# A GraphSAGE layer pair on one core: the first eight edge groups of layer 1 gathered from x, and other loop ends

## The chip, the core and the metric

The kernel runs on one core of a Trainium2 chip. Its time is that of the device, in microseconds (us), as the median of several runs. A core has five engines with a queue of instructions each: TensorE (PE, with its weight loads shown apart as PEld), VectorE (DVE), ScalarE (ACT), GpSimd (POOL) and SyncE (SP). SP and ACT also issue DMAs, and so does POOL: its indirect DMAs gather rows of a table in DRAM by a list of indices. One profiled execution stands beside the runs.

## The reference

Nodes have 128 features; N is 12500 nodes, E is 200000 edges, sorted by destination.

```python
h    = jnp.maximum(_layernorm(x), 0.0)
w    = edge_weight_raw / jnp.maximum(wsum, EPS)[dst]
feat = jax.nn.relu(node_features @ W_pool + b_pool)
msg  = feat[src] * w[:, None]
neigh = jax.ops.segment_max(msg, dst, num_segments=N)
rst  = node_features @ W1_self + neigh @ W1_neigh + b1
h    = jax.nn.relu(rst / jnp.maximum(norm(rst), EPS))
neigh2 = segment_sum(h[src] * w[:, None], dst) / jnp.maximum(deg, 1.0)[:, None]
out  = jax.nn.relu(h @ W2_self + neigh2 @ W2_neigh + b2)
return x + out
```

Here `node_features` is the first `h`. Layer 1 takes, for each node, the largest message of its edges; layer 2 takes their sum.

## The kernel before

The kernel has three parts, and each is an order of instructions written out by hand.

**Preparation** (L426 to L473). x is held in SBUF in 98 tiles of 128 nodes, and a step works on four of them. Four stages of different steps lie in one turn of the loop: statistics of the layer norm on DVE (L462, L463), then the normalised rows with relu on ACT and their transposes on PE (L451, L453), then hT (the node features with features on partitions) and the product with W_pool (L438, L441), and last the table `feat`: bias on DVE (L430), relu on POOL (L433), store to `feat_d` in DRAM by SP (L434). `fr` has three buffers, so a relu waits for the store of three steps before. The loads of x are in SP's queue ahead of those stores. POOL also clears the SBUF that x leaves (L454). `edges1` prepares the weights and segment limits of 65536 edges at a time, `sources` the indices `srcT` (L410 to L417).

**Layer 1** (L646 to L760). Edges go in 391 groups of 512, the last one of 320. `gather` (L561) issues four indirect DMAs for a group, of 128 rows each, from `feat_d` into one of eight `gt` buffers. Every twelfth group has its first 128 rows fetched row by row by SP and ACT instead (class `Rows`, L501), in the eleven steps ahead of it; its `takes` says which groups. Step i of the loop scales the rows of group i by edge weight on ACT (L696), and PE transposes them to the PSUM tile `pm` (L697). For group i-1 DVE runs a scan over the 512 edges (L703), which takes the running maximum within each destination; `kt`, a row of `keep_d` broadcast to 128 partitions, restarts it where the destination changes. Two edges are joined into one (L711, L712), transposed back (L740), copied (L727), and for group i-4 a product with a selection matrix (L752) puts the last edge of each destination into a window of 48 nodes, `pa`, which ACT copies into `agg` (L745). The PSUM tile `pa` has one buffer. `turns` says at which step a tile of 128 nodes is complete; `nodes1` (L597) then multiplies it by W1_self and W1_neigh, normalises it, and stores it to `h_d`. Background work of the edges fills the loop by `side_step`.

**Layer 2** (L763 to L807) gathers from `h_d` in the same groups; every eighth has rows by SP and ACT. PE multiplies the gathered rows by a matrix of weights (L801), DVE adds the window to `agg` (L806), and `nodes2` ends with bias, relu, the addition of x and the store.

A gather is only issued when its `gt` buffer has been read by the group eight before it. A gather from `feat_d` also waits for all stores of that table, and one from `h_d` for all of that one.

What decides which group is taken row by row, and where a gather stands in POOL's queue:

```python
def takes(self, g):
    return g % self.every == 0 and self.every <= g < NG - 4
...
for j, k in chunks:
    if j == 0 and byrow and byrow.takes(g):
        continue
    nc.gpsimd.indirect_dma_start(
        out=gt[:k, j, :], out_offset=None, in_=table_d[:, :],
        in_offset=bass.IndirectOffsetOnAxis(ap=srcT[:k, t, j, r:r + 1], axis=0))
```

Of the kernel before, what the change touches and what calls it, by code (L numbers as in the profile page):

```python
# [18 lines left out]
P = 128  # L19
D = 128  # L20
# [10 lines left out]
BL = 8  # L31
XC = 8


@with_exitstack
def gnn_kernel(ctx, tc, x, src, dst, ew, w_pool, b_pool, w1s, w1n, b1, w2s, w2n, b2, out):
# [22 lines left out]
    RHO = N * G / E  # L59
    assert TAIL > 0 and TAIL % Q == 0 and E % SLOW_B == 0 and D == x.shape[1]  # L60

# [24 lines left out]
    rp = both.enter_context(tc.tile_pool(name="rows", bufs=1))  # L86
    gp = both.enter_context(tc.tile_pool(name="eg", bufs=8))
    prep = ExitStack()
# [55 lines left out]
    for t0 in range(2 * Q, HI, XC):  # L144
        load_x(t0, XC)

    def load_rest():
# [262 lines left out]
    def sources():  # L410
        for t in range(NT):
# [5 lines left out]
            yield  # L417


    first_edges = edges1(pq, 0)  # L420
    source_steps = sources()
    rest = load_rest()
    groups = list(node_groups())
    offs, rstds, pts, pfs = ({} for _ in range(4))
    for i in range(len(groups) + 3):
        at = [groups[i - k] if 0 <= i - k < len(groups) else None for k in range(4)]  # L426
        if at[3]:
            t0, n = at[3]
            fb = wk.tile([P, Q, D], F32, name="fb")
            nc.vector.tensor_tensor(fb[:, :n, :], pfs.pop(i - 3)[:, :n, :],  # L430
                                    bp_all[:, None, :].to_broadcast([P, n, D]), OP.add)
            fr = wk.tile([P, Q, D], F32, name="fr", bufs=3)
            nc.gpsimd.tensor_scalar(fr[:, :n, :], fb[:, :n, :], 0.0, None, op0=OP.max)  # L433
            nc.sync.dma_start(feat_d[t0 * P:(t0 + n) * P, :].rearrange("(q p) d -> p q d", p=P),  # L434
                              fr[:, :n, :])
        if at[2]:
            t0, n = at[2]
            nc.scalar.activation(hT[:, t0:t0 + n, :], pts.pop(i - 2)[:, :n, :], AF.Copy)  # L438
            pf = pfs[i - 2] = ps.tile([P, Q, D], F32, name="pf")
            for q in range(n):  # L440
                nc.tensor.matmul(pf[:, q, :], hT[:, t0 + q, :], W["pool"], start=True, stop=True)  # L441
        if at[1]:
# [27 lines left out]
        if i >= 6:  # L470
            next(rest, None)
        if i >= len(groups) - 4:
            next(source_steps, None)  # L473
    for steps in (first_edges, rest, source_steps):
        for _ in steps:
            pass
# [13 lines left out]

    def edges_of(g):

        ne = G if g < GF else TAIL
        return *divmod(g, P), ne, [(j, min(P, ne - j * P)) for j in range(-(-ne // P))]

    def pairs_of(g):
# [4 lines left out]
    class Rows:  # L501
# [5 lines left out]

        def __init__(self, pool, table_d, every, share):
            self.pool, self.every, self.share = pool, every, share
            self.bytes = table_d[:, :].bitcast(U8).rearrange("n b -> (n b)")  # L510
            self.tiles, self.index, self.plan = {}, {}, {}
            self.ri = pool.tile([64, P], I32, name="ri", bufs=1)
            assert sum(n for _, n, _ in share) == P
            for g in range(every, NG - 4, every):
                first = g - every - 1
                at = 0
                for eng, n, rb in share:
                    for s in range(n // rb):
                        turn = max(first + s * every // (n // rb), 0)
                        self.plan.setdefault(turn, []).append((g, eng, at, rb))  # L520
                        at += rb
            self.turn(-2)
            self.turn(-1)

        def takes(self, g):
            return g % self.every == 0 and self.every <= g < NG - 4

        def turn(self, i):

            for g, lead, step in ((i + self.every + 2, -1, self.shift), (i + self.every + 3, -2, self.load)):  # L530
                if i == lead:
                    step(self.every)
                elif i >= 0 and g > self.every and self.takes(g):
                    step(g)
# [25 lines left out]

    def gather(pool, table_d, g, byrow=None):  # L561
        t, r, ne, chunks = edges_of(g)
        gt = pool.tile([P, Q, D], F32, name="gt")
        for j, k in chunks:
            if j == 0 and byrow and byrow.takes(g):
                continue
            nc.gpsimd.indirect_dma_start(  # L567
                out=gt[:k, j, :], out_offset=None, in_=table_d[:, :],
                in_offset=bass.IndirectOffsetOnAxis(ap=srcT[:k, t, j, r:r + 1], axis=0))
        return gt  # L570

    def turns(behind):
# [19 lines left out]

    def linear(po, t, nT, self_w, neigh_w):
        nc.tensor.matmul(po, hT[:, t, :], W[self_w], start=True, stop=False)
        return nc.tensor.matmul(po, nT, W[neigh_w], start=False, stop=True)  # L595

    def nodes1(wk, ps, t, nT, store=True):  # L597

        po = ps.tile([P, D], F32, name="pn")
        linear(po, t, nT, "1s", "1n")  # L600
        yield
# [28 lines left out]
    def nodes2(wk, ps, t, nT, xr):  # L630

        po = ps.tile([P, D], F32, name="pn")
        linear(po, t, nT, "2s", "2n")
        yield
# [11 lines left out]
    with tc.manual_schedule(), tc.tile_pool(name="ew", bufs=3) as wk, \  # L646
            tc.tile_pool(name="ep", bufs=2, space=PSUM) as ps:
        AHEAD = 4
        jobs = [(due, job(lambda: ps.tile([P, Q, P], F32, name="pq", bufs=1), t)) for due, job, t in background()]
# [9 lines left out]

        gts, kts, pms, scs, sels, prs, rws, pas = ({} for _ in range(8))  # L660
        turn = turns(6)
        busy = {}

        def keep_rows(g):
            ne = edges_of(g)[2]
            kts[g] = wk.tile([P, G], BF16, name="kt", bufs=AHEAD + 3)
            nc.sync.dma_start(kts[g][:, :ne], keep_d[g:g + 1, :ne].to_broadcast([P, ne]))  # L667

# [6 lines left out]

        for g in range(AHEAD):
            keep_rows(g)
        carry = NEG
        byrow = Rows(wk, feat_d, 12, [(nc.sync, 96, 8), (nc.scalar, 32, 4)])
        for i in range(max(turn) + 6):  # L680
            byrow.turn(i)
            byrow.rows(i, nc.sync)
            node_stage(5)
            if i + AHEAD < NG:
                keep_rows(i + AHEAD)
            if i < NG:
                gts[i] = gather(gp, feat_d, i, byrow)

            if i < NG:
                t, r, ne, chunks = edges_of(i)  # L690
                gs = wk.tile([P, Q, D], F32, name="gs", bufs=2)
                pms[i] = ps.tile([P, G], F32, name="pm")
                gt = gts.pop(i)
                for j, k in chunks:
                    rows_j = byrow.tile(i) if j == 0 and byrow.takes(i) else gt[:k, j, :]
                    nc.scalar.activation(gs[:k, j, :], rows_j, AF.Copy, scale=ewT[:k, t, j, r:r + 1])  # L696
                    nc.tensor.transpose(pms[i][:, j * P:j * P + k], gs[:k, j, :], ident[:k, :k])  # L697

            g = i - 1
# [29 lines left out]
            node_stage(4)  # L729
            if i in turn:  # L730
                n = turn[i]
                st = nodes1(wk, ps, n, agg[:, n * P:(n + 1) * P])
                next(st)
                busy[i + 1, 1] = st
            g = i - 2
            if 0 <= g < NG:
                prs[g] = ps.tile([P, Q // 2, D], F32, name="pr")
                sc = scs.pop(g)
                for j, k in pairs_of(g)[3]:
                    nc.tensor.transpose(prs[g][:k, j, :], sc[:, j * P:j * P + k], ident)  # L740

            g = i - 5
            if 0 <= g < NG:
                at = window_at(mybir.EngineType.Activation, g)
                nc.scalar.activation(agg[:, bass.ds(at, LW)], pas.pop(g), AF.Copy)  # L745
            g = i - 4
            if 0 <= g < NG:
                chunks = pairs_of(g)[3]
                pas[g] = ps.tile([P, LW], F32, name="pa", bufs=1)
                rows, sel = rws.pop(g), sels.pop(g)  # L750
                for j, k in chunks:
                    nc.tensor.matmul(pas[g], rows[:k, j, :], sel[:k, j, :], start=j == 0,  # L752
                                     stop=j == len(chunks) - 1)
            node_stage(2)
            byrow.rows(i, nc.scalar)
            if i % 3:
                side_step()
# [5 lines left out]
    with tc.manual_schedule(), tc.tile_pool(name="ew2", bufs=3) as wk, \  # L763
            tc.tile_pool(name="ep2", bufs=3, space=PSUM) as ps:
        iota = ps.tile([P, LW], F32, bufs=1)
        nc.vector.tensor_copy(iota, cols[:, 0, :])
        nc.vector.memset(agg, 0.0)
        gts, ss, pas, xrs = ({} for _ in range(4))
        turn = turns(3)
        late = None  # L770
        byrow = Rows(wk, h_d, 8, [(nc.sync, 64, 8), (nc.scalar, 64, 8)])
        for i in range(max(turn) + 2):
# [22 lines left out]
            if 0 <= g < NG:  # L795
# [3 lines left out]
                for j, k in chunks:  # L799
                    rows_j = byrow.tile(g) if j == 0 and byrow.takes(g) else gt[:k, j, :]  # L800
                    nc.tensor.matmul(pas[g], rows_j, s[:k, j, :], start=j == 0,  # L801
                                     stop=j == len(chunks) - 1)
            g = i - 2
            if 0 <= g < NG:
# [123 lines left out]
```

## Time and profile before

| | us |
|---|---|
| median of 3 runs | 3939.56 (3939.38 to 3942.92) |
| the profiled execution | 3936.91 |
| its span | 3935.1 |
| first gather from feat_d | 95.30 |
| last gather from feat_d | 2007.19 |
| first gather from h_d | 2033.27 |
| last gather from h_d | 3923.95 |

A line of the page's groups names the program line, the engine and operation, what is written and read, the shape and the number of instructions; behind the first bar come the busy time and the mean of one in ns, behind the second the idle time of the engine ahead of it and what ended it. In the timeline a line has its start, its duration, and in square brackets how long its engine was idle before and what ended that. "issue" is time in which an engine waited for nothing that the profile shows. A gather's time on POOL ends before its rows land: the last one of layer 2 starts on POOL at 3923.95, is over there at 3924.85, and PE reads its rows at 3926.31.

### The profile page before, as it was taken

How to read it: one execution, taken by the hardware profiler on the slowest of the kernel's cores; microseconds unless marked ns; L12 is line 12 of the kernel's file. 1: busy time of each engine (PE TensorE's matmuls, PEld its weight loads, DVE VectorE, ACT ScalarE, POOL GpSimd, SP SyncE). 2: the span in 40 equal slices, each digit the busy share in tenths (PEclk: the TensorE clock that was granted, in tenths of full speed). 3: DMA queues.
4: the chain of work that ended last, by engine and by line, in shares of the span. 5: the costliest groups of instructions: out<-in, count | busy, mean ns of one | idle time of the engine just before them, and what ended most of it. 6: DMA issues, size and time to landing. Idle time of an engine off the chain costs nothing.

```text
span 3935.1 us, 55137 instructions
## 1 busy us (share of the span) xinstructions
PE 2156.9 (55%) x8349; PEld 1760.9 (45%) x8349; DVE 1664.5 (42%) x4708; ACT 808.7 (21%) x2947; POOL 2925.7 (74%) x3105
## 2 busy tenths in 40 slices
PE   6446546555556545545545555555555555555555
PEld 4335435444445434444444444444444444444444
DVE  7556656666656656655652222122122222122221
ACT  6334334334334334334320000000000000000000
POOL 5777777777777777777757777777777777777776
PEclk8555565555555555555555555555555555555555
DMA  6233333333333333333322222222222222222222
GB/s 168 76 85 84 86 86 85 85 85 84 85 85 84 85 85 84 85 85 84 84 61 62 63 62 61 62 62 62 62 62 63 62 62 61 62 62 62 62 62 58
DMA packets 245792, 295.43 MB, mean 75 GB/s; under 512 B 71023, under 2 KB 195518, under 8 KB 245424
## 3 DMA queue, kind: packets, MB, share of 16 engines
q0 software_dynamic: 97472, 199.75, 18.7%
q1 hardware_dynamic: 139024, 89.04, 8.5%
q10 hardware_dynamic: 8928, 3.03, 0.3%
q14 instruction: 296, 2.42, 0.2%
q8 instruction: 72, 1.18, 0.1%
HBM read 271.77 MB, written 19.77 MB: 74 GB/s over the span
## 4 chain that ended last, share of the span: by engine, by line
DMA 23%; POOL 23%; issue 17%; SPq 9%; PE 9%; DVE 8%; ACT 5%; ACTq 5%; POOLq 0%; DVEq 0%
POOL gt L567 23%; DMA gt<-h_d,srcT 14%; SPq L556 6%; PE pm L697 4%; DVE pm L703 4%; ACTq L556 3%; DMA ga<-feat_d 3%; DMA kt<-keep_d 3%; ACT gs L696 3%; SPq L552 2%; DMA ri<-in_src 1%; ACTq L552 1%; PE pa L752 1%; DMA gt<-feat_d,srcT 1%; SPq L667 1%
## 5 line engine op out<-in xcount | busy, mean ns | idle before, releaser
L567 POOL DMA_INDIRECT gt<-feat_d,srcT x1531 | 1446.1, 945 | 469.5 <-issue 376.4
L567 POOL DMA_INDIRECT gt<-h_d,srcT x1515 | 1429.5, 944 | 487.3 <-issue 389.5
L801 PE MATMUL pa<-s,gt 128*128 128x48 f32 x3030 | 966.6, 423 | 827.6 <-DMA gt<-h_d,srcT 736.2
L801 PEld LDWEIGHTS pa<-s,gt 128*128 128x128 f32 x3030 | 757.0, 312 | 1038.5 <-DMA gt<-h_d,srcT 819.5
L697 PE MATMUL pm<-ident,gs 128*128 128x128 f32 x1563 | 481.2, 440 | 896.0 <-DVE sc L712 472.8
L697 PEld LDWEIGHTS pm<-ident,gs 128*128 128x128 f32 x1563 | 287.3, 197 | 1030.0 <-ACT gs L696 471.0
L806 DVE TENSOR_TENSOR agg<-pa,agg 128x48 f32 x391 | 81.2, 208 | 1438.8 <-PE pa L801 1025.2
L703 DVE TENSOR_TENSOR_SCAN pm<-kt,carry,pm 128x512 f32<-128x512 bf16 x390 | 498.6, 1279 | 231.3 <-PE pm L697 116.9
L696 ACT ACTIVATE gs<-gt,ewT 128x128 f32<-128x128 f32 x1531 | 495.6, 391 | 269.0 <-DMA ga<-feat_d 187.7
L752 PEld LDWEIGHTS pa<-sel,rows 128*128 128x128 f32 x1564 | 352.5, 311 | 35.9 <-ACT agg L745 34.4
L752 PE MATMUL pa<-sel,rows 128*128 128x48 f32 x1564 | 356.6, 374 | 3.5 <-ACT agg L745 1.2
L740 PE MATMUL pr<-ident,sc 128*128 128x128 f32 x782 | 236.2, 403 | 1.9 <-DVE sc L712 1.9
L542 DVE TENSOR_SCALAR ri<-ri 1x128 int32<-1x128 int32 x80 | 18.6, 233 | 512.3 <-DMA ri<-in_src 504.7
L720 DVE TENSOR_SCALAR sel<-cols,lastT,invT 128x48 f32<-128x48 f32 x782 | 211.4, 324 | 0.0
L712 DVE COPY_PREDICATED sc<-kt,pm 128x256 f32<-128x256 int16 x391 | 172.9, 442 | 13.3
L740 PEld LDWEIGHTS pr<-ident,sc 128*128 128x128 f32 x782 | 163.4, 218 | 2.2 <-issue 1.3
L711 DVE COPY sc<-pm 128x256 f32<-128x256 f32 x391 | 162.0, 414 | 0.0
L783 DVE TENSOR_TENSOR s<-hit,w2T 128x192 f32<-128x192 f32 x391 | 139.8, 357 | 13.5
L727 ACT ACTIVATE rows<-pr 128x256 f32<-128x256 f32 x392 | 142.3, 363 | 2.6 <-PE pr L740 2.4
L781 DVE TENSOR_TENSOR hit<-iota,locT 128x192 f32<-128x192 f32 x391 | 139.1, 356 | 0.8
L745 ACT ACTIVATE agg<-pa 128x48 f32 x391 | 78.6, 201 | 169.1 <-PE pn L595 164.8
L607 ACT ACTIVATE sq<-r 128x128 f32<-128x128 f32 x98 | 29.8, 304 | 401.9 <-DVE r L603 401.9
(149 smaller groups left out, 1395.7 us busy)
## 6 DMA issues: line engine op xcount, KB each, us to landing
kt<-keep_d SPq DMA_DIRECT2D x390, 128.0 KB
ga<-feat_d SPq DMA_DIRECT2D x3072, 0.5 KB
ga<-h_d SPq DMA_DIRECT2D x3072, 0.5 KB
ga<-h_d ACTq DMA_DIRECT2D x3072, 0.5 KB
gt<-feat_d,srcT POOLq DMA_INDIRECT x1531
gt<-h_d,srcT POOLq DMA_INDIRECT x1515
ga<-feat_d ACTq DMA_DIRECT2D x1024, 0.5 KB
h_d<-h SPq DMA_DIRECT2D x98, 64.0 KB
```

The costliest lines, as they stand in the source:

```text
L556: eng.dma_start(ga[r + k:r + k + 1, :], self.bytes[None, bass.ds(at[k], 4 * D)])
L567: nc.gpsimd.indirect_dma_start(out=gt[:k, j, :], out_offset=None, in_=table_d[:, :], in_offset=bass.IndirectOffsetOnAxis(ap=srcT[:k, t, j, ...
L696: nc.scalar.activation(gs[:k, j, :], rows_j, AF.Copy, scale=ewT[:k, t, j, r:r + 1])
L697: nc.tensor.transpose(pms[i][:, j * P:j * P + k], gs[:k, j, :], ident[:k, :k])
L703: nc.vector.tensor_tensor_scan(pm[:, :ne], kt[:, :ne], pm[:, :ne], carry, op0=OP.add, op1=OP.max)
L711: nc.vector.tensor_copy(sc[:, :ne // 2], two[:, :, 1])
L712: nc.vector.copy_predicated(sc[:, :ne // 2], new[:, :, 1], two[:, :, 0])
L720: nc.vector.tensor_scalar(sels[g][:k, j, :], cols[:k, 1, :], lastT[:k, t, j, r:r + 1], invT[:k, t, j, r:r + 1], op0=OP.is_equal, op1=OP.mult)
L727: nc.scalar.activation(rws[g][:k, j, :], pr[:k, j, :], AF.Copy)
L740: nc.tensor.transpose(prs[g][:k, j, :], sc[:, j * P:j * P + k], ident)
L752: nc.tensor.matmul(pas[g], rows[:k, j, :], sel[:k, j, :], start=j == 0, stop=j == len(chunks) - 1)
L801: nc.tensor.matmul(pas[g], rows_j, s[:k, j, :], start=j == 0, stop=j == len(chunks) - 1)
```

## The change

Groups 0 to 7 of layer 1 no longer use the table. During the preparation POOL gathers the rows of x themselves for their edges, two gathers in each step from step 2 on, into the eight `gt` buffers. These rows then go through layer norm, relu, transpose, the product with W_pool, bias and relu by themselves, as [feature x edge] tiles: group 0 at the end of the preparation, groups 1 to 7 in the first steps of layer 1. The edge weights come as rows broadcast to all partitions, and DVE multiplies by them. So gathers from `feat_d` begin with group 8. To have indices at that time, `sources` runs its first pass in steps 0 and 1.

```diff
+    bp_col = rp.tile([P, 1], F32)
+    nc.sync.dma_start(bp_col, b_pool[:, None])
...
+    def raw_stats(r):
+        mv = rp.tile([P, Q, 2], F32, name="raw_mv", bufs=2)
+        for q in range(Q):
+            st = rp.tile([P, 6], F32, name="raw_st", bufs=2)
+            nc.vector.bn_stats(st, gts[r][:, q, :])
+            nc.vector.bn_aggr(mv[:, q, :], st)
+        rstd = rp.tile([P, Q], F32, name="raw_rstd", bufs=2)
+        nc.scalar.activation(rstd, mv[:, :, 1], AF.Sqrt, bias=eps)
+        raws[r] = mv, rstd
+
+    def raw_rows(get, r):
+
+        mv, rstd = raws.pop(r)
+        nc.vector.reciprocal(rstd, rstd)
+        off = rp.tile([P, Q], F32, name="raw_off", bufs=2)
+        nc.vector.scalar_tensor_tensor(off, mv[:, :, 0], -1.0, rstd, op0=OP.mult, op1=OP.mult)
+        pt = raws[r] = get()
+        for q in range(Q):
+            nc.scalar.activation(gts[r][:, q, :], gts[r][:, q, :], AF.Relu, bias=off[:, q:q + 1],
+                                 scale=rstd[:, q:q + 1])
+            nc.tensor.transpose(pt[:, q, :], gts[r][:, q, :], ident)
+
+    def raw_product(get, r):
+
+        nc.scalar.activation(gts[r], raws.pop(r), AF.Copy)
+        pf = raws[r] = get()
+        nc.tensor.matmul(pf.rearrange("p q n -> p (q n)"), W["pool"],
+                         gts.pop(r).rearrange("p q n -> p (q n)"), start=True, stop=True)
...
-        if i >= len(groups) - 4:
+        if i == 1:
+            bias_rows = split_bias()
+        if i < 2 or i >= len(groups) - 4:
             next(source_steps, None)
+        if i >= 2:
+            n = 2 if i < len(groups) else len(raw_chunks)
+            for r, j in raw_chunks[:n]:
+                gts[r] = gather(gp, x, r, only=j, gt=gts.get(r))
+            raw_chunks = raw_chunks[n:]
+        k = i - len(groups)
+        if k == 1:
+            raw_rows(pq, 0)
+        if k == 2:
...
+        if k in (0, 1):
+            raw_stats(k)
```

The table's bias goes to PE: `split_bias` splits b_pool into three bf16 parts on DVE once (eight small operations), and one matmul of three rows adds them in PSUM ahead of the product. The relu leaves POOL: DVE does it, in every fourth step ACT, straight from PSUM to `fr`.

```diff
-            fb = wk.tile([P, Q, D], F32, name="fb")
-            nc.vector.tensor_tensor(fb[:, :n, :], pfs.pop(i - 3)[:, :n, :],
-                                    bp_all[:, None, :].to_broadcast([P, n, D]), OP.add)
+            pf = pfs.pop(i - 3)
             fr = wk.tile([P, Q, D], F32, name="fr", bufs=3)
-            nc.gpsimd.tensor_scalar(fr[:, :n, :], fb[:, :n, :], 0.0, None, op0=OP.max)
+            if i % 4 == 3:
+                nc.scalar.activation(fr[:, :n, :], pf[:, :n, :], AF.Relu)
+            else:
+                nc.vector.tensor_scalar(fr[:, :n, :], pf[:, :n, :], 0.0, None, op0=OP.max)
...
+            nc.tensor.matmul(pf[:, :n, :], ones_r[0:3, :P], bias_rows[0:3, :n, :], start=True, stop=False)
             for q in range(n):
-                nc.tensor.matmul(pf[:, q, :], hT[:, t0 + q, :], W["pool"], start=True, stop=True)
+                nc.tensor.matmul(pf[:, q, :], hT[:, t0 + q, :], W["pool"], start=False, stop=q == n - 1)
```

In layer 1 the first eight steps take the raw groups, with `pq` as the one PSUM tile for their transposes and products:

```diff
+        weight_rows(0)
+        keep_rows(0)
+        keep_rows(2)
         carry = NEG
-        byrow = Rows(wk, feat_d, 12, [(nc.sync, 96, 8), (nc.scalar, 32, 4)])
+        byrow = Rows(wk, feat_d, 12, [(nc.sync, 96, 8), (nc.scalar, 32, 4)], 24, NG - 16)
...
+            if i < FIRST:
+                pm = pms[i] = ps.tile([P, G], F32, name="pm")
+                w = ws.pop(i).rearrange("p q n -> p (q n)")
+                if i == 0:
+                    nc.vector.tensor_tensor(pm, gts.pop(0).rearrange("p q n -> p (q n)"), w, OP.mult)
+                else:
+                    nc.scalar.activation(pm, raws.pop(i).rearrange("p q n -> p (q n)"), AF.Relu, bias=bp_col)
+                    nc.vector.tensor_tensor(pm, pm, w, OP.mult)
+                if i + 1 < FIRST:
+                    weight_rows(i + 1)
+                    raw_rows(pq, i + 1)
...
+            if i + 1 < FIRST:
+                raw_product(pq, i + 1)
+            if i + 2 < FIRST:
+                raw_stats(i + 2)
```

Rows by SP and ACT are now for groups 24, 36 and so on up to 372. `keep_rows` loads two groups' rows with one DMA, every second step. At the end of layer 1 the window copies of the last steps move ahead of other work, a node tile is begun after the window's product rather than before, `pa` of every second of the last groups lies in the `pq` bank, and the W1_self halves of the last two node tiles run ahead of their turn into a bank of their own. In layer 2 the set-up of `Rows` moves ahead of the clearing of `agg`, and the W2_self halves of the last two tiles are computed at step NG - 1:

```diff
+                if g >= NG - 5 and g % 2 and not jobs:
+                    pas[g] = ps.tile([P, Q, P], F32, name="pq", bufs=1)[:, 0, :LW]
+                else:
+                    pas[g] = ps.tile([P, LW], F32, name="pa", bufs=1)
...
+            if i >= NG - 2:
+                begin_node()
+            n = HI - 2 + i - NG
+            if n in (HI - 2, HI - 1) and turn.get(i + 5) == n:
+                own[n] = ps.tile([P, G], F32, name="pm")[:, :D]
+                linear_own(own[n], n, "1s")
...
+            if i == NG - 1:
+                for n in (HI - 2, HI - 1):
+                    own[n] = ps.tile([P, D], F32, name="pn")
+                    linear_own(own[n], n, "2s")
```

## The prediction

> **What bounds the kernel now.** I read the page first, then POOL in order of time, then the stretches where POOL has no gather. The page's parts 1 and 5:
>
> ```profile
> span 3935.1 us, 55137 instructions
> PE 2156.9 (55%) x8349; PEld 1760.9 (45%) x8349; DVE 1664.5 (42%) x4708; ACT 808.7 (21%) x2947; POOL 2925.7 (74%) x3105
> ...
> L567 POOL DMA_INDIRECT gt<-feat_d,srcT x1531 | 1446.1, 945 | 469.5 <-issue 376.4
> L567 POOL DMA_INDIRECT gt<-h_d,srcT x1515 | 1429.5, 944 | 487.3 <-issue 389.5
> ```
>
> POOL is busiest, and almost all of it is gathers of 945 ns with about 0.30 us of "issue" before each. The timeline of POOL, with first and last gathers of layer 1 and the first of layer 2, shows whether anything interrupts them:
>
> ```profile
> 95.30 1.16 POOL L567 DMA_INDIRECT gt<-feat_d,srcT  x1 [2.75 <-DMA feat_d<-fr]
> 96.77 0.94 POOL L567 DMA_INDIRECT gt<-feat_d,srcT  x1 [0.30 <-issue]
> ```
> ```profile
> 2007.19 0.91 POOL L567 DMA_INDIRECT gt<-feat_d,srcT  x1 [0.30 <-issue]
> 2033.27 0.95 POOL L567 DMA_INDIRECT gt<-h_d,srcT  x1 [25.17 <-DMA ri<-in_src]
> ```
>
> From 95.30 to 2007.19 there are 1530 steps: 1.2496 us each, which is duration plus issue and nothing else. Layer 2, 2033.27 to 3923.95, gives 1.2488 over 1514 steps. So the span is five terms: 95.3 of preparation, 1531 gathers, a hole of 25.17, 1515 gathers, 10.25 of tail. Only what changes one of these counts; work on DVE, ACT and PE inside a layer is covered as long as it frees the eight gt buffers (8 x 4 x 1.25 = 40 us ahead).
>
> **Gathers removed from layer 1.** Groups 0 to 7 leave the loop: 32 gathers. Rows by sync and scalar are now taken for groups 24 to 372 (30) instead of 12 to 384 (32), which gives 2 back. 1531 - 32 + 2 = 1501, so 30 x 1.2496 = **-37.5**. Layer 2 takes the same groups as before.
>
> **The 32 gathers in the preparation.** From step 2 on, two per step: 2.5 us beside a 0.52 us memset is 3.0 of a step of about 3.3 (reciprocals of rstd at 17.68, 20.94, 24.27), and the relu of 1.49 us leaves POOL. They end at step 17 of 27, and only raw_stats at step 25 reads them, so they are hidden with seven steps to spare. Their traffic is not quite free: the DMA share is 0.95 to 1.09 until 30 us, while x is loaded at 301 GB/s, and some 8 gathers of 64 KB fall there: 0.5 MB, 1.7 us later for the loads and all that SP has queued behind them.
>
> Here the Trainium skill speaks against the change. Its page "SBUF — State Buffer", section "A bandwidth-pool intuition that's wrong (but worth ruling out)", says that descriptors of a DMA from GpSimd wait while a VectorE operation in a two-port mode holds the shared port: 3100 ns for one that takes 620 alone. Gathers now go beside the DVE-heavy preparation. By that figure a step would hold 2 x 3.4 + 0.5 = 7.3 us, 16 steps 117 us, and the first gather of the table would come near 130 instead of 103: the whole gain gone. The row says otherwise: layer 1 has 782 tensor_scalars SBUF to SBUF in f32 (sel, 324 ns), of the kind that the page names, beside 1531 gathers of median 944 and at most 1179 ns. I take the row.
>
> **Preparation, its end.** DVE, ACT and the waits of SP up to 95 us:
>
> ```profile
> L462 DVE BATCH_NORM_STATS2 st<-agg 128x6 f32<-128x128 f32 x98 | 26.1, 266 | 0.9 <-DMA agg<-in_x 0.9
> L463 DVE BATCH_NORM_AGGREGATE mv<-st 128x2 f32<-128x6 f32 x98 | 17.8, 182 | 3.4
> L430 DVE TENSOR_TENSOR fb<-pf,b 128x512 f32<-128x512 f32 x24 | 16.3, 681 | 6.2 <-PE pt L453 2.5 <-POOL fr L433 2.4 <-PE pf L441 1.3
> ```
> ```profile
> 30.18 1.48 POOL L433 TENSOR_SCALAR fr<-fb 128x512 f32<-128x512 f32 x1 [6.62 <-DMA feat_d<-fr]
> ```
>
> DVE sets the pace (17.98 us busy of 20 from 40 to 60). The reader sees at 30.18 that the fourth fr waited for the first feat_d store, which SP issues at 26.00, behind the x loads. POOL took this wait before, and DVE only 2.4 us of it. Now DVE writes fr itself and meets it at step 6. It gets there about 24.4 (23.67 before, + 1.4 for split_bias, which is 8 small operations, about 2.0 us less a 0.6 idle, - 0.65 for a relu on ACT). The store comes 1.7 + 0.4 (bp_col) later, lands near 32.2, and fr ends at 33.0. Step 8 before ended at 32.4; now 33.0 + 5.7 - 0.65 = 38.1: **+5.7**. From there every fourth relu goes to ACT, which has 5 us of 20 free: four times 0.65, of which I count 2.0: **-2.0**. The bias matmul goes to PE, which waits for ACT there: nothing (at most 25 x 0.3 if PE were late). At the end the relu on POOL (1.48) goes, but the sqrt of raw_stats(0) stands ahead of the last hT on ACT, and four raw relus (1.65) ahead of the last fr: the store is issued near 93.7 rather than 92.6: +1.1. The table is complete at 94.66 + 4.8 = 99.5.
>
> **A new wait at the start of layer 1.** The buffer of gather 8 is gts[0], read by DVE in group 0 together with weight_rows(0), whose place in SBUF is free only when the last feat_d store has landed. So: 99.5, + 2.7 for 256 KB (kt lands in 2.9 to 3.1 in the chain), + 0.67 multiply, + 0.2 = 103.1. First gather: **+7.8** in all. Behind it on POOL is every gather. Bounds: +3.5 (no DVE stall at step 6) and +13.
>
> **The raw groups as a pace.** Gather g for 9 to 15 waits until raw group g - 8 is through its matmul. One loop of it: four relus 1.65, transpose 0.45, copy 0.65, matmul of 512 columns in two passes (pf: 8 x 128 columns in 1.16 at full clock, 1.8 at the granted 0.53), relu 0.65, hops 0.3, multiply and scales 1.0: 6.5. By DVE: stats 4 x 0.40, scan with its copies 2.2, sel 0.5, multiply and scales 1.0, sqrt and relu on ACT between 1.0: 6.3. POOL needs 5.0. Gathers 10 to 15 wait 1.5 each: 6 x 1.5 = 9, with a little at the start **+9.5**. Bounds 0 (hops overlap) and 28 (a pace of 9). Afterwards the loop needs about 3.3 to 4.4 us a group and catches up.
>
> **The hole between the layers.** 25.17 before. In the timeline ACT waits for rows by sync of group 384 so long that six groups stand behind it when POOL ends at 2008.10:
>
> ```profile
> 2000.22 0.40 ACT L696 ACTIVATE gs<-ga,ewT 128x128 f32<-128x128 f32 x1 [15.11 <-DMA ga<-feat_d]
> ```
>
> The last gs begins at 2014.19; without a backlog it would at 2008.1 + 1.5, so 4.6 go. Then the order at the end: window copies ahead, pa in two banks, own products of the last two node tiles early. Counted down the dependences: gs, transpose, scan, copies 4.0 after POOL's end, pr, rows, pa, copy 6.7, two products, r, norm, h, store 12.8. Queues in between I put at 3: 16, **-9.2** (bounds 13 and 21). Pairs of keep rows halve their issues (0.36 each on SP), hidden. In layer 2 the set-up of the rows by sync moves ahead of the 10.55 us memset on DVE; DVE is the consumer there and POOL is 40 us ahead, so this is nothing; without that cover it would be a gain, since those rows could start 10 us earlier. The eight weight loads of 256 KB stand in SP's queue between keep rows; their price shows only in the first, above.
>
> **Tail.** PE runs 2s before 2n for two tiles after the last add; the first halves go ahead: **-0.65** of 10.25.
>
> **Sum.** +7.8 + 9.5 - 37.5 - 9.2 - 0.65 = -30.0; span 3905.1. The profiled execution took 3936.91 (span + 1.8), the median of the runs is 3939.56; I put the difference to the median: **3909.5**.
>
> **Rivals.** (a) The start hides better: first gather +4, raw groups +2, hole 16: -41, **3898**. For it: ACT and PE have slack; against: SP's queue and the single pq bank are serial. (b) Raw groups at 9 us, POOL held 28 instead of 9.5: **3928**. For it: eight hops between three engines in each, and two queues with work between; against: the rows sum to 6.5. (c) Slower: the same place, one mechanism. DVE and ACT wait for each other within a raw group (sqrt in ACT's queue ahead of the relu that DVE waits for), and the single pq makes transposes and product strictly serial; at 12 us a group POOL is held 49: **3949**. It decides from 5 + 39.5 / 7 = 10.6 us on; twice as many hops as I count would be needed. (d) The change does not do what it says: srcT of the first rows late, or gathers held by the port: the start moves to 130 and about 3 is gained, **3937**.
>
> **Chances.** Forecast (3898 to 3920) 0.58; (a) 0.12; (b) 0.17; (d) and the like 0.05; (c) 0.08. A change of 0.2% (8 us) is about what can be told from none. Faster 0.87, within 0.05, slower 0.08. Range 3893 to 3927.
>
> **What would show it.** 1501 gathers of feat_d at 1.25; first of them at 103; 32 gathers of x at 944 ns between 13 and 65; waits of POOL for PE before gathers 10 to 15 of 1.5 us; a hole of 16; 10.25 to 9.6 at the end. Wrong it is if POOL waits after group 16, or if the raw groups take 9 us and more.

## The result and the profile after

| | kernel before | changed kernel |
|---|---|---|
| median, us | 3942.49 (6 runs, 3939.38 to 3947.13) | 3922.11 (6 runs, 3919.01 to 3924.24) |
| ratio | | 0.9945, interval 0.9935 to 0.9955 |
| profiled execution, us | 3936.91 | 3919.01 |
| its span, us | 3935.1 | 3917.2 |

The changed kernel is 0.55% faster: 20.4 us between the medians, 18.0 us between the two spans (3935.14 and 3917.18). The forecast was 30.

The page of the changed kernel, parts 1 and 5. The columns are those of the page before.

```profile
span 3917.2 us, 54274 instructions
PE 2182.0 (56%) x8390; PEld 1775.6 (45%) x8390; DVE 1675.8 (43%) x4795; ACT 826.5 (21%) x2978; POOL 2898.7 (74%) x3082
...
L434 POOL DMA_INDIRECT gt<-h_d,srcT x1515 | 1433.2, 946 | 478.9 <-issue 402.0
L434 POOL DMA_INDIRECT gt<-feat_d,srcT x1501 | 1421.0, 947 | 478.9 <-issue 350.7
```

POOL is still the busiest engine, with the 1501 gathers of `feat_d` that were counted. Its timeline (start, duration, engine, line; in brackets the idle time before and what ended it) shows the five terms of the span again: preparation, gathers, hole, gathers, tail.

```profile
103.15 0.95 POOL L434 DMA_INDIRECT gt<-feat_d,srcT  x1 [9.98 <-DVE raw_off L458]
...
115.09 0.95 POOL L434 DMA_INDIRECT gt<-feat_d,srcT  x1 [1.99 <-PE pq L469]
...
149.22 0.95 POOL L434 DMA_INDIRECT gt<-feat_d,srcT  x1 [2.22 <-PE pq L469]
...
1992.09 0.91 POOL L434 DMA_INDIRECT gt<-feat_d,srcT  x1 [0.30 <-issue]
2009.62 0.96 POOL L434 DMA_INDIRECT gt<-h_d,srcT  x1 [16.62 <-issue]
```

The table of `feat` is gathered from 103.15 on. At seven places from gather group 9 to 15 POOL then stands for PE (`pq` L469, the product of a raw group). Normal idle before a gather is 0.30, so each bracket less 0.30 is lost: 0.25 at group 9, 1.69 three times, 1.92 three times, 11.1 us together. After 149.22 POOL waits for no other engine in layer 1. The hole is 16.62 in place of 25.17.

With both traces the difference of the spans can be written out, term by term:

| term | forecast, us | traces, us | how the trace gives it |
|---|---|---|---|
| start of the table's gathers | +7.8 | +7.85 | 103.15 - 95.30 |
| raw groups as a pace | +9.5 | +11.1 | the seven waits |
| 30 fewer gathers | -37.5 | -37.5 | 30 x 1.2496 |
| hole between the layers | -9.2 | -8.55 | 16.62 - 25.17 |
| tail | -0.65 | +1.8 | from the end of the last gather to the end of the span: 12.12 against 10.29 |
| step from gather to gather | 0 | +7.3 | layer 1 without its waits 1.2519 against 1.2496, layer 2 1.2513 against 1.2488, over 1500 and 1514 steps |
| sum | -30.0 | -18.0 | |

So the waits and counts that were named are there, most of them in their sizes. Most of the 12 us that are missing stand in two rows that the forecast held at nothing or had with the other sign: the step of the gathers and the tail.

**The gathers of x in the preparation.** POOL's timeline, the first and the last of the 32:

```profile
15.82 1.11 POOL L434 DMA_INDIRECT gt<-in_x,srcT  x1 [0.17 <-issue]
...
70.73 0.94 POOL L434 DMA_INDIRECT gt<-in_x,srcT  x1 [0.30 <-issue]
```

After the first one they take 0.94 to 0.95 us each, beside DVE's work of the preparation, and are over at 71.7. The first `raw_stats` reads such rows at 91.82.

**The start.** First SP's queue, then DVE's, from the timeline:

```profile
13.91 13.63 SPq L136 DMA_DIRECT2D agg<-in_x  x8
27.59 0.36 SPq L148 DMA_DIRECT2D bp_col<-in_L_gnn_b_pool  x1
28.05 0.39 SPq L505 DMA_DIRECT2D feat_d<-fr  x1
```
```profile
32.67 0.69 DVE L504 TENSOR_SCALAR fr<-pf 128x512 f32<-128x512 f32 x1 [7.49 <-DMA feat_d<-fr]
```

These rows show the queue in which the first store of the table waits: the last of the loads of x, then `bp_col`, then the store, at 28.05. The fourth `fr` has to wait for that store's buffer. It was POOL that stood there before; now it is DVE, idle for 7.49 us, with the statistics of all later tiles behind it. At the other end of the preparation DVE's multiplication for raw group 0 waits for the weight rows, whose load SP issues at 98.70. SP's queue and DVE's there:

```profile
98.70 0.35 SPq L779 DMA_DIRECT2D gs<-in_edge_weight  x1
```
```profile
102.18 0.70 DVE L805 TENSOR_TENSOR pm<-gt,gs 128x512 f32<-128x512 f32 x1 [6.17 <-DMA gs<-in_edge_weight]
```

The first gather follows at 103.15.

### The profile page after: what moved, and what is told of

Read it like the earlier page. It is cut to its first block, busy times and chain, and to the rows that moved or that the text cites. A ratio compares the mean times of both kernels' runs of the same rounds, so it can differ in the third digit from the quotient of the medians.

```text
span 3917.2 us, 54274 instructions
## 1 busy us (share of the span) xinstructions
PE 2182.0 (56%) x8390; PEld 1775.6 (45%) x8390; DVE 1675.8 (43%) x4795; ACT 826.5 (21%) x2978; POOL 2898.7 (74%) x3082
## 5 line engine op out<-in xcount | busy, mean ns | idle before, releaser
L434 POOL DMA_INDIRECT gt<-feat_d,srcT x1501 | 1421.0, 947 | 478.9 <-issue 350.7
L821 PE MATMUL pm<-ident,gs 128*128 128x128 f32 x1531 | 462.2, 434 | 836.0 <-DVE sc L838 472.7
L820 ACT ACTIVATE gs<-gt,ewT 128x128 f32<-128x128 f32 x1501 | 480.0, 391 | 190.9 <-DMA ga<-feat_d 166.2
```

Of the source, the lines that this page charges most:

```text
L434: nc.gpsimd.indirect_dma_start(out=gt[:k, j, :], out_offset=None, in_=table_d[:, :], in_offset=bass.IndirectOffsetOnAxis(ap=srcT[:k, t, j, ...
```

## The experiments

The experiments were run in two sets. The runs of one set share a chip and the runs of the kernel before there. In all of them the line that matters is POOL's: first gather, waits, step, hole, tail.

### First set: the kernel before, the changed one, six buffers for `fr`, six raw groups

Two edits of the changed kernel. The first gives DVE buffers enough to pass step 6 without a store having landed:

```diff
-            fr = wk.tile([P, Q, D], F32, name="fr", bufs=3)
+            fr = wk.tile([P, Q, D], F32, name="fr", bufs=6)
```

The second has six raw groups but keeps eight `gt` buffers, so that two gather groups find a free buffer:

```diff
-FIRST = 8
+FIRST = 6
...
-    gp = both.enter_context(tc.tile_pool(name="eg", bufs=FIRST))
+    gp = both.enter_context(tc.tile_pool(name="eg", bufs=8))
```

The kernel before:

> The kernel before, profiled once more. In the first two profiles a step from gather to gather took 1.2496 and 1.2488 us before, and 1.2519 (without the seven waits) and 1.2513 after, which is 7 us over 3016 gathers. Theory A, the step differs from chip to chip or run to run: here, on another run, it moves by 1 to 3 ns in both layers with no change of the kernel. Theory B, the change makes gathers slower (more traffic, another place in SBUF): it is again 1.2496 and 1.2488 within 0.5 ns. The stretch from the last VectorE instruction to the end of the span was 5.5 before and 7.8 after; by A it also moves here.

The changed kernel:

> The changed kernel once more, beside the kernel before on one chip. Both theories: 20 us faster than before. A: its step is within 0.5 ns of that of the kernel before in this same call. B: 2.5 ns above it.

Six buffers for `fr`:

> Six buffers of fr instead of three, so that VectorE doesn't wait for the first store of the table at step 6 (7.49 us in the trace of after). Theory: this wait is what moved the end of the preparation, so the first gather of feat_d comes at 97 to 99 instead of 103.15, and the time falls by 4 to 6 us against the changed kernel. Rival: the preparation is then held by ACT and PE, and the first gather comes at 101.5 or later, under 1.7 us gained.

Six raw groups:

> Six raw groups instead of eight, with eight gt buffers as before; so groups 6 and 7 are gathered from the table into free buffers. Theory (raw groups at 6.7 us each pace POOL, and gather 8 waited for the weights of group 0): first gather of feat_d at about 99.5, waits of POOL for PE under 1.5 us in sum instead of 11.0, 1509 gathers instead of 1501: +10.0 - 3.7 - 9.6 = 3.3 us faster than the changed kernel. Rival (a wait of POOL early is made good later, since the rest of the layer has slack): the 8 gathers more cost their 10 us and little comes back, 5 to 10 us slower than the changed kernel.

Measured, on a chip where the kernel before took 1.48 times as long and the others about as much more:

| | median, us | ratio to the kernel before | first gather from feat_d, us |
|---|---|---|---|
| before (9 runs; profiled 5825.76) | 5829.63 | | 94.33 |
| changed (4 runs) | 5764.53 | 0.9879 (0.983 to 0.993) | 105.08 |
| six `fr` | 5758.38 | 0.9866 (0.983 to 0.9902) | 100.32 |
| six raw groups | 5776.25 | 0.9914 (0.9886 to 0.9942) | 101.17 |

The page of the kernel before on that chip, part 5:

```profile
L567 POOL DMA_INDIRECT gt<-feat_d,srcT x1531 | 1445.3, 944 | 1503.2 <-ACT rows L727 1000.5
L567 POOL DMA_INDIRECT gt<-h_d,srcT x1515 | 1429.5, 944 | 1317.4 <-PE pa L801 555.4
```

A gather takes 944 ns, as in the first trace of this kernel (945 and 944). What grew is the idle time before it, from 469.5 to 1503.2 us in layer 1 and from 487.3 to 1317.4 in layer 2: POOL stands for ACT's copy of `rows` and for PE's product, and those engines in turn show single waits of up to 22 and 36 us. SP, which issues rows one by one, is slower too. Eight rows from its queue on this chip, one of the long cases, and then in the first trace:

```profile
1008.56 11.20 SPq L556 DMA_DIRECT2D ga<-feat_d  x8
```
```profile
1002.27 2.53 SPq L556 DMA_DIRECT2D ga<-feat_d  x8
```

The register moves between these DMAs (6144 on SP, with no wait on them) take 868 us in sum here and 178 us in the first trace, and SP stands 722 us idle in front of some of them, against 16. Why that is so on this chip is not settled; the kernel before has it as well, so it is not the change's. The times of this set therefore say little of the single terms, and their intervals overlap. Two things can be read. The preparation lies ahead of most of it: six `fr` buffers bring the first gather 4.8 us forward. And so can the gather itself. The page of the changed kernel on this chip:

```profile
L434 POOL DMA_INDIRECT gt<-feat_d,srcT x1501 | 1416.5, 944 | 1475.8 <-ACT rows L853 970.4
L434 POOL DMA_INDIRECT gt<-h_d,srcT x1515 | 1429.3, 943 | 1304.5 <-PE pa L934 570.1
```

The step of the gathers had two theories (A: the longer step belonged to the execution or the chip; B: the change brings it). In the trace beside the result the added time is in the gather itself, 947 and 946 ns against 945 and 944, while the usual idle time before it is 0.30 us in both. The changed kernel on this chip is back at 944 and 943. That is theory A, shown with the changed kernel itself.

### Second set: the same two edits, no raw groups, the old order at the end

This set ran on a chip where the kernel before takes 3937.12 us (13 runs, 3933.11 to 3943.33). The changed kernel itself is not in it; the kernel with the old order at the end is nearest to it.

Six buffers for `fr`, and six raw groups, as above:

> Six buffers of fr, as in e1_fr6, where a gather had gaps of 10 us all through both layers, which no kernel explains (the kernel before took 5826 us there); this call is meant for the sums. Against the kernel before on the same chip the changed kernel took 0.9945. Theory (VectorE's wait at step 6 moved the end of the preparation): first gather of feat_d 4.8 us earlier, as in e1_fr6, and ratio 0.9932 to 0.9935. Rival (the start is made good later): ratio 0.9945.

> Six raw groups with eight gt buffers. Theory (raw groups pace POOL and only the seventh and eighth make it wait): first gather of feat_d at 99.5, waits of POOL for PE under 1.5 us, 1509 gathers: 3.3 us faster than the changed kernel, ratio 0.9937. Rival (the waits are made good): 5 to 10 us slower than the changed kernel, ratio 0.9958 to 0.9970.

No raw groups at all. The relu and the bias stay where the change put them, and so do the rows by SP and ACT and the order at the ends:

```diff
-FIRST = 8
+FIRST = 0
...
-    gp = both.enter_context(tc.tile_pool(name="eg", bufs=FIRST))
+    gp = both.enter_context(tc.tile_pool(name="eg", bufs=8))
...
-        k = i - len(groups)
-        if k == 1:
-            raw_rows(pq, 0)
...
-        weight_rows(0)
```

> No raw groups: all groups come from the table, 1533 gathers of feat_d (rows by sync from group 24 to 372); bias by PE, loop ends and layer 2 as in the changed kernel. Theory: preparation 96 to 97 (without raw work at its end, still with the wait at step 6), no waits for PE, hole 16.6 as in the changed kernel: +1.5 + 2.5 - 8.5 - 0.7 = 5 us faster than before, ratio 0.9987, and the raw groups alone are worth 15 us. Rival (the ends are worth little and the raw groups all): within 2 us of before, hole over 20.

The old order of the last steps of layer 1, with everything else of the change kept, the rows by SP and ACT up to group 372 too:

```diff
-            if i < NG - 2:
-                begin_node()
+            begin_node()
...
-            if i < NG - 2:
-                window_copy(i - 5)
+            window_copy(i - 5)
...
-                if g >= NG - 5 and g % 2 and not jobs:
-                    pas[g] = ps.tile([P, Q, P], F32, name="pq", bufs=1)[:, 0, :LW]
-                else:
-                    pas[g] = ps.tile([P, LW], F32, name="pa", bufs=1)
+                pas[g] = ps.tile([P, LW], F32, name="pa", bufs=1)
...
-            if n in (HI - 2, HI - 1) and turn.get(i + 5) == n:
-                own[n] = ps.tile([P, G], F32, name="pm")[:, :D]
-                linear_own(own[n], n, "1s")
```

> The changed kernel with the order of the last steps of layer 1 as before (window copies, begin of a node tile, one pa buffer, no products ahead), rows by sync still ending with group 372. Theory (the hole had two parts: 4.6 us of backlog from the rows by sync, and 4 from the order): hole 20.5 to 21.5, 4 to 5 us slower than the changed kernel, ratio 0.9956. Rival A (backlog alone): hole 16 to 17.5. Rival B (order alone): hole 24 to 25.

Measured. "Waits" are POOL's waits for PE at the raw groups, beyond 0.30; "hole" is the idle time in front of the first gather from `h_d`; "end" is the time from the end of VectorE's last operation to the end of the span. The steps are without waits. The first two rows are the traces already shown.

| | median, us | ratio to the kernel before | first gather | waits | gathers of feat_d | hole | step, layer 2 | end |
|---|---|---|---|---|---|---|---|---|
| before | | | 95.30 | 0 | 1531 | 25.17 | 1.2488 | 5.5 |
| changed | | 0.9945 (0.9935 to 0.9955) | 103.15 | 11.1 | 1501 | 16.62 | 1.2513 | 7.7 |
| six `fr` | 3909.08 | 0.992 (0.9904 to 0.9937) | 98.75 | 11.1 | 1501 | 17.77 | 1.2487 | 7.8 |
| six raw groups | 3909.32 | 0.9921 (0.9904 to 0.9937) | 100.01 | 1.2 | 1509 | 17.35 | 1.2488 | 7.6 |
| no raw groups | 3932.99 | 0.9989 (0.998 to 0.9999) | 96.74 | 0 | 1533 | 16.55 | 1.2486 | 6.9 |
| old order at the end | 3915.68 | 0.994 (0.9923 to 0.9957) | 103.09 | 11.1 | 1501 | 18.64 | 1.2487 | 7.6 |

Six `fr` buffers and six raw groups came out a little faster than expected (0.9932 to 0.9935 and 0.9937). Those ratios were counted from the changed kernel's, whose profiled execution has the longer step.

**The step of the gathers is not the change's (theory A).** The kernel with the old order at the end has the change's layer 2 and nearly all of its layer 1. Its gathers of `h_d` come every 1.2487 us, and those of `feat_d`, without the waits, every 1.2493. All four kernels of this set show 1.2486 to 1.2488 in layer 2, and the changed kernel's gathers took 944 and 943 ns in the first set. So the 2.3 to 2.5 ns more per gather in the profiled execution of the changed kernel were that execution's or its chip's: 7.3 us of the span. What made them is not known. That the kernel before took 5.4 us more in the runs beside the result (3942.49) than on this chip points the same way, without showing it.

**The stall of DVE at step 6** is one cause of the later start. POOL's and DVE's timelines with six `fr` buffers:

```profile
98.75 0.95 POOL L434 DMA_INDIRECT gt<-feat_d,srcT  x1 [10.30 <-DVE raw_off L458]
```
```profile
26.20 0.69 DVE L504 TENSOR_SCALAR fr<-pf 128x512 f32<-128x512 f32 x1 [0.19 <-PE pf L513]
...
33.72 0.69 DVE L504 TENSOR_SCALAR fr<-pf 128x512 f32<-128x512 f32 x1 [1.97 <-PE pf L513]
```

No `fr` waits for a store any more, and the table's gathers begin 4.3 us earlier than with three buffers on the same chip (98.75 against 103.09). Not all of that is kept. In the same trace POOL meets waits in mid layer that the others do not have, five of 0.4 to 0.9 us beyond the 0.30, such as this one, with ACT's side of it below:

```profile
1110.62 0.94 POOL L434 DMA_INDIRECT gt<-feat_d,srcT  x1 [1.21 <-ACT rows L853]
```
```profile
1109.07 0.40 ACT L820 ACTIVATE gs<-ga,ewT 128x128 f32<-128x128 f32 x1 [5.61 <-DMA ga<-feat_d]
```

ACT waited 5.61 us for rows that SP and ACT fetch one by one, and POOL stood behind ACT. Those five places cost 2.7 us in all, and the hole 1.1 more than in the changed kernel.

**The raw groups' pace** goes with the number of free buffers. With six groups and eight buffers POOL waits once:

```profile
136.17 0.94 POOL L434 DMA_INDIRECT gt<-feat_d,srcT  x1 [1.52 <-PE pq L469]
```

1.2 us in place of 11.1, for which eight more gathers are paid, 10.0 us. That is nothing won or lost; the kernel gains by its first gather, at 100.01 in place of 103.09.

**Without raw groups** the first gather comes at 96.74, 1.4 us after that of the kernel before. POOL and DVE:

```profile
96.74 1.11 POOL L434 DMA_INDIRECT gt<-feat_d,srcT  x1 [4.82 <-DMA feat_d<-fr]
```
```profile
30.59 0.69 DVE L504 TENSOR_SCALAR fr<-pf 128x512 f32<-128x512 f32 x1 [4.20 <-DMA feat_d<-fr]
```

The stall of DVE at step 6 is there without any raw group, 4.20 us long, and comes with the relu on DVE; with raw groups it is 5.50 us on this chip (old order at the end) and 7.49 in the first trace. So without raw groups the change costs 1.4 of the 7.85 us: the relu and the bias, with the `bp_col` load in SP's queue, and the early pass of `sources`, which this kernel still has. The raw groups cost the other 6.4. Against the kernel with the old order at the end, 103.09, they split in two: the last store of the table is issued 2.5 us later (96.49 against 93.95), and from that store to the first gather it is 6.6 us instead of 2.8, with the weight rows and the multiplication between. All of the change but the raw groups is worth 0.11% (ratio 0.9989, an interval that just leaves 1 out): in its trace the hole gives 8.6 us, and the start (1.4), two more gathers of `feat_d` (2.5) and the tail (1.0) take most of that back. That is as expected (0.9987, hole 16.6). The raw groups bring the rest: on the same chip the time is 17.3 us shorter with eight of them, the old order at the end included, and 23.7 us shorter with six, than with none; 15 were expected.

**The hole** was put down half to a backlog of ACT and half to the order of the last steps. The point between them is DVE's scan of the last group, of 320 edges. The timelines of the kernel before, of the one with the old order at the end, and of the changed one:

```profile
2018.76 0.88 DVE L703 TENSOR_TENSOR_SCAN pm<-kt,carry,pm 128x320 f32<-128x320 bf16 x1
```
```profile
1992.15 0.89 DVE L825 TENSOR_TENSOR_SCAN pm<-kt,carry,pm 128x320 f32<-128x320 bf16 x1 [0.37 <-PE pm L819]
```
```profile
1995.39 0.89 DVE L829 TENSOR_TENSOR_SCAN pm<-kt,carry,pm 128x320 f32<-128x320 bf16 x1 [0.16 <-PE pm L821]
```

And POOL around the hole with the old order:

```profile
1988.11 0.90 POOL L434 DMA_INDIRECT gt<-feat_d,srcT  x1 [0.30 <-issue]
2007.64 0.96 POOL L434 DMA_INDIRECT gt<-h_d,srcT  x1 [18.64 <-issue]
```

POOL's last gather of layer 1 ends at 2008.10, 1989.01 and 1993.00. So the last scan follows it by 10.66 us in the kernel before, by 3.14 with the old order, and by 2.39 in the changed kernel. Of the 8.55 us that the hole lost, 7.5 go in front of that scan with the old order still in place, and 1.0 of them is given back behind it. The new order is worth 2.0 against the changed kernel's trace (18.64 - 16.62), and 0.9 to 2.1 against the three kernels of the same set that have it (17.77, 17.35 and 16.55). Steadier is the stretch from the start of the last scan to the first gather of `h_d`: 15.49 us with the old order, 14.1 to 14.2 in all four traces with the new one, so 1.3 us. The times do not show it: the ratio with the old order, 0.994, is no worse than that of the changed kernel. The hole of 18.64 lies between the ranges expected for both parts (20.5 to 21.5) and for the backlog alone (16 to 17.5).

That the 7.5 come from the rows by SP and ACT ending at group 372 is read from ACT. Its last wait for such rows ends 7.9 us before POOL's last gather does in the kernel before, and 57 us before it with the old order (12.01 us long, ended at 1932.09); its last scaling starts 6.1 us after POOL's end before, and 1.3 with the old order. A kernel with the rows alone put back was not run, and that one link stays argued.

**The end.** From the end of DVE's last operation to the end of the span it is 5.5 us before, and 6.9 to 7.8 in the five kernels with the change's tail. In the first set it is 5.9 before, and 7.7 to 7.9 in the three others. The timeline of the changed kernel and then of the one before:

```profile
3909.16 0.29 DVE L721 SCALAR_TENSOR_TENSOR o<-o,xr 84x128 f32<-84x128 f32 x1
```
```profile
3929.33 0.29 DVE L638 SCALAR_TENSOR_TENSOR o<-o,xr 84x128 f32<-84x128 f32 x1
```

The DMA view (queue, kind: packets, MB, share) of the last 5.0 us of the changed kernel, and of the last 4.0 us of the one before:

```profile
q14 instruction: 3, 0.02, 1.7%
q8 instruction: 1, 0.02, 1.4%
```
```profile
q14 instruction: 3, 0.02, 1.7%
q8 instruction: 1, 0.02, 1.4%
q1 hardware_dynamic: 7, 0.00, 0.3%
```

The queue `q1` carries the output rows. In the kernel before, the last of them move within the last 4 us; in the changed kernel none moves in the last 5.0. What moves there are packets of instructions. SP's own records in the traces show where the difference lies. After the last store SP jumps over the part of the program that does not run and stands there for 2.5 to 2.7 us, in the kernel before as in the others. Then it goes through a row of semaphore operations, one every 0.06 to 0.1 us. In all eight traces with the change's tail it stops once more within that row, for 1.4 to 1.7 us; in the two traces of the kernel before it does not. In the changed kernel this stop (1.68) and a last store whose issue takes 1.05 us instead of 0.56 are the 2.2 us. It is no chance of one execution. That SP stops there for instructions to be loaded fits the packets, but is not shown, and which part of the program makes it so was not tried.

## Why the prediction came out right, and where its terms were off

The time was forecast at 3909.5 and measured at 3922.11, inside the range of 3893 to 3927; the likeliest case's own range ended at 3920. The direction, the bound (POOL's gathers) and the division of the span into five terms were right. The sizes of the start, the gathers removed, the raw groups and the hole came within 2 us; the tail had the wrong sign, and one term was missing.

- **Start, +7.8 against +7.85.** The stall of DVE at step 6 was forecast with the end of `fr` at 33.0; it ends at 33.36. Six `fr` buffers remove the stall and 4.3 us of the start, which leaves 98.75, the +3.5 that the forecast gave as the bound without a stall. The second wait, for the weight rows, was forecast to release the first gather at 103.1, and did so at 103.15. That it fits to 0.05 us is luck. Behind step 6 the delay is 7.2 us and not 5.7 (`rstd` of the eighth step at 39.55 against 32.31), and more of it is made good than was forecast; and SP issues the weight rows at 98.70, 0.8 earlier than forecast, while DVE gets them 3.5 us later instead of 2.7.
- **The shared port.** The 32 gathers of x took 0.95 us on average, as every other gather, and the first gather of `feat_d` did not move to 130. That estimate had taken 3100 ns as the price of every gather. The same section of the Trainium skill ("SBUF — State Buffer", "A bandwidth-pool intuition that's wrong (but worth ruling out)") gives the rule as blocked until the VectorE operation ends, plus about 115 ns. The operations of this preparation are short, 0.27 us for the statistics and 0.69 for the relu, so an estimate by that rule holds up a gather by less than 0.9 us. The row of layer 1 gave the right answer, but its operations (`sel`) are not those of the preparation. Whether any operation here holds the port is shown by no run.
- **Raw groups, +9.5 against +11.1.** The pace was worked out at 6.5 us a group; it is 6.69 to 6.92. The product of a raw group was put at 1.8 us and takes 2.08, in this row of PE's timeline, where the granted clock was 0.50:

```profile
106.06 2.08 PE L469 MATMUL pq<-gt,w_pool 128*128 128x512 f32 x2 [0.69 <-ACT gt L467]
```

The trace of before had this size: there the product with W_pool for four tiles took 1.16 us in most places, and 2.07 at 35.69, where the granted clock was 0.50. The rivals of 9 and 12 us a group were far off.
- **Gathers removed, -37.5.** The count is exact, 1501. The price of the others was taken from one execution to the nanosecond: over 3016 gathers, 2.4 ns each are 7.3 us, more than any other error here. This is the largest part of the miss, and by both sets no effect of the change. The range was wide enough to hold it, but was not drawn for it.
- **Hole, -9.2 against -8.55.** The sum came out well because two sizes were off against each other: 4.6 for the backlog and 4.6 for the order were forecast; up to the scan of the last group the old order shows 7.5 (6.5 of the hole), and the new order gives 1.3 behind the scan. The forecast read the backlog at the last `gs` on ACT (2014.19 - 2009.6), which leaves out what was queued behind it on PE and DVE.
- **Tail, -0.65 against +1.8.** The part that was forecast, from the last gather's end to DVE's last operation, went from 4.77 to 4.38, -0.4. The step that failed is that what follows was taken as fixed; it grew by 2.2, of which SP's second stop is 1.7.

With the gathers of the changed kernel at the step of before, its span would be 3917.2 - 7.3 = 3909.9, against 3905.1 forecast; tail (2.5), raw groups (1.6) and hole (0.65) are those 4.8.

Two kernels of the second set, six `fr` buffers and six raw groups, stand at ratios of 0.992 and 0.9921, the changed kernel at 0.9945. These come from different sets and their intervals touch, so that they beat the change is likely and not shown. To do both, or to issue the last loads of x behind the first store of the table, was not tried.

## What to carry to other kernels

When one queue sets the span, write the span as start, count times step, holes and end, and fill each from the trace: the large terms then come out within 2 us, and what is left is the step's own change from run to run, which has to stand in the range (2.4 ns in 1.25 us were 7 us here). An engine that takes over an operation takes over its waits: the relu carried the wait for a store buffer from an engine with time to the one that set the pace. When work is made by several engines per buffer, compare its pace with the consumer's and count how many buffers are free ahead; two more of them were worth as much as eight gathers.

## What the runs showed of the hardware that was not expected

- The same gather loop of layer 2 stepped at 1.2486 to 1.2488 us in five traces and at 1.2513 in one, with no wait that the trace names: the 2.5 ns are in the gather's own time.
- On one chip the kernel before took 1.48 times as long (5829.63 us against 3937.12 on another), with gathers still of 944 ns. There SP's register moves between row DMAs took 868 us in sum instead of 178, and all engines had idle stretches.
- The last 5 us of the changed kernel hold four packets of instructions and no data. The end of a program is part of its time, and is not the same for two programs that end with the same operations: 5.5 and 5.9 us in two traces of the kernel before, 6.9 to 7.9 in eight with the change's tail.
